# Unordered token scatters, expert tokens and rows on GpSimd's DMA queue, and first weights staged in the K and V tiles

## The chip, the cores and the metric

The kernel runs on one core of a Trainium2 chip. A core has five engines that run side by side, each with its own instruction queue, which it works off in order: TensorE (PE, matrix multiplication), VectorE (DVE), ScalarE (ACT), GpSimd (POOL) and SyncE (SP, which issues DMAs). Waits between engines are made with semaphores. The metric is the device time of one execution in microseconds; a smaller time is better. The kernel before was run three times: 2608.23, 2605.57 and 2600.91 us, median 2605.57.

## The reference

One layer of a perceiver works on 512 tokens of width 512, in three parts, each with a layer norm ahead of it and a residual sum behind it:

```python
x = x + xattn(layernorm(x), ctx_1024)   # 16 heads of 64, 512 queries, 8192 keys
x = x + attn(layernorm(x))              # Mamba block (conv, scan over tokens), then an MLP of width 2048
x = x + ffn(layernorm(x))               # experts
```

The experts' part is the one at the end:

```python
logits = x @ router_w.T
top_vals, top_idx = top_k(logits, 2)           # each token goes to 2 of 16 experts
gates = sigmoid(top_vals)
h = silu(x @ gate[e]) * (x @ up[e])            # width 512
moe = sum over a token's two experts of gates * (h @ down[e])
shared = (silu(x @ sg) * (x @ su)) @ sd        # width 1024, for every token
```

## The kernel before

Every fp32 operand is split into two fp16 parts, high and low, and a product is made of three fp16 matmuls. ACT makes the high part and VectorE the low one, so each weight block costs one instruction on each of them (`split_w`, lines 176 and 177; `pieces`, lines 1094 and 1095).

**The start and the first pass of attention.** The keys and values are made in four passes of two head pairs each (`filler`, line 426), over 16 chunks of 512 context rows. In the first pass a chunk's context arrives in fp32 (`ctx_first`, line 224: two halves named `cf`, tag `p32` with three buffers), is split, written back to DRAM, and used for K of two head pairs (`kproj_units`) and V (`vproj_units`). `smax_units` makes scores of the chunk's keys with the queries and keeps their running maximum: per chunk 16 matmuls into PSUM, each emptied by ACT (line 305). Their generators lie in the list `side`, and `pump` puts one unit of them between every four units of K and V. In pass 0 the block at line 452 loads the first weights: Wk of pair 0 into `wst`, Wk of pair 1 and Wv into buffers of tag `p32`, Wq into buffers of tag `t2k`. `first_norm` (layer norm of x, transposes) and the query projections `qproj` stand behind chunk 0 (line 483). The three biases are the first loads of the program (lines 163 to 165). TensorE's order is the program's own here (a manual schedule); the other engines' order and the DMA issues are arranged by the planner of the framework, which goes by when it expects operands to be ready. The attention proper follows, with passes 1 to 3 of this filler between its matmuls, then the Mamba block and the MLP (`tail`).

The tags `k` (two buffers) and `v` (three) in the pool `L` hold the key and value blocks of the attention proper (`main_load`, line 338); the first of these loads comes at 96 us of the profiled execution.

**The experts.** When the router's choice is known, each of the 1024 (token, expert) pairs has a slot in the DRAM buffer `xd_d`: 16 blocks of 128 rows for the experts and 7 for overflow. Eight indirect DMAs on GpSimd scatter the tokens' rows (2 KB each) to their slots (line 1201). They write to one tensor, so the framework orders each behind the one before. Meanwhile TensorE works on the shared part (`ffn(..., RS, ...)`, weights `rsg`, `rsu`, `rsd` loaded at line 761 into five buffers of tag `wpm`). Then `moe` goes over 16 experts and two overflow blocks: `moe_in` loads a block of 128 tokens (`xd`, three buffers, line 1208) and transposes it, `moe_up` makes gate and up, `moe_turn` transposes the result, `moe_down` makes the rows and writes them to `y_d` (line 1257). `moe_in` of the next block stands behind `moe_up`, `moe_down` of a block behind the `moe_up` of the next. Weights come in pieces of 512 KB (`wef`, six staging buffers, line 1089), six per expert, and are split into `we` (18 buffers) and `wpm`. All of these loads and the writes to `y_d` are in SyncE's queue. At the end a branch decides on further overflow blocks (line 1280), and eight indirect DMAs on GpSimd gather the rows of each token (line 1285), which VectorE weights and adds.

Of the kernel before, what the change touches and what calls it, by code (L numbers as in the profile page):

```python
# [9 lines left out]
F32 = mybir.dt.float32  # L10
AF = mybir.ActivationFunctionType
ALU = mybir.AluOpType
# [4 lines left out]
P = 128  # L17
NQ = 512
DM = 512
NC4 = DM // P  # L20
NPAIR = 8
CH = 512
NCH = 8192 // CH
NT = CH // P
WS = 16.0
# [4 lines left out]
NPASS = NPAIR // 2  # L30
# [8 lines left out]
def perceiver_layer(ctx: ExitStack, tc: tile.TileContext, a: dict, out: bass.AP):  # L39
    nc = tc.nc  # L40
# [22 lines left out]
    y_d = scr.tile([(16 + NOV) * P, DM], F32, name="y_d")  # L63
    xd_d = scr.tile([(16 + NOV) * P, 2 * DM], F16, name="xd_d")
# [70 lines left out]
    L = R(late, "late", 1)  # L135
    sb1 = R(attn, "a1", 1)
    sb2 = R(attn, "a2", 2)
# [12 lines left out]
    for i in range(NQT):  # L150
        t = (L if i == (NPAIR - 1) % NQT else sb1).tile([P, 2, NQ], F16, name=f"qlm{i}")
# [8 lines left out]
    bq_sb = sb1.tile([P, NPAIR], F32, name="bq_sb")  # L160
    bk_sb = sb1.tile([P, NPAIR], F32, name="bk_sb")
    bv_sb = L.tile([P, NPAIR], F32, name="bv_sb")
    nc.sync.dma_start(bq_sb, a["bq"])
    nc.sync.dma_start(bk_sb, a["bk"])
    nc.sync.dma_start(bv_sb, a["bv"])
    nc.vector.tensor_scalar(bk_sb, bk_sb, WS, None, ALU.mult)

    def stage_w(src, n, tag, stage=("wst", 1), bufs=2):
        st = sb2.tile([P, NC4, n], F32, name=f"wst_{tag}", tag=stage[0], bufs=stage[1])
        nc.sync.dma_start(st, src)  # L170
        return lambda: split_w(st, n, tag, bufs)

# [7 lines left out]
    def load_w(*x, **k):  # L180
        return stage_w(*x, **k)()
# [21 lines left out]
    def qproj(p, w):  # L203
        wh, wl = w
        ps = bank_j([P, NQ], F32, f"psq{p}")
        mm3(ps, lambda i: wh[:, i, :], lambda i: wl[:, i, :], lambda i: xTh[:, i, :], lambda i: xTl[:, i, :], NC4)
        q32 = sb2.tile([P, NQ], F32, name="q32", tag="t2k", bufs=4)
        nc.scalar.activation(q32, ps, AF.Identity, bias=bq_sb[:, p : p + 1], scale=1.0 / WS)
        qh = sb2.tile([P, NQ], F16, name="qh", bufs=4)
        ql = sb2.tile([P, NQ], F16, name="ql", bufs=2)  # L210
        split_dve(qh, ql, q32)
        return qh, ql
# [74 lines left out]
    def smax_units(c, i, qh, kh, runm, wide):  # L287

        if c == 0:
            runm[i] = sb2.tile([P, 4, 2, CH], F16, name=f"runm{i}", tag=f"runm{i}", bufs=1)  # L290
        for q2 in range(2):
            sf = sb3.tile([P, 2, 2, CH], F16, name="sf", bufs=2)
            pss = []
            for qi in range(2):
                qt = 2 * q2 + qi
                for hh in range(2):
                    s = slice(hh * 64, hh * 64 + 64)
                    pool, tag = (ps_s, "pss") if wide and qi else (ps_x, "px")
                    ps = pool.tile([P, CH], F32, name="psx", tag=tag)
                    nc.tensor.matmul(ps, lhsT=qh[s, qt * P : (qt + 1) * P], rhs=kh[s, 0, :], start=True, stop=True)  # L300
                    pss.append((sf[:, qi, hh, :], ps))
                if wide and not qi:
                    continue
                for dst, ps in pss:
                    nc.scalar.activation(dst, ps, AF.Copy, scale=1.0 / (8.0 * WS))  # L305
                pss = []
                if not qi:
                    yield 406
            r = runm[i][:, 2 * q2 : 2 * q2 + 2]
            if c == 0:  # L310
                nc.vector.tensor_copy(r, sf)
            else:
                nc.vector.tensor_tensor(r, r, sf, ALU.max)  # L313
            yield 626 if wide else 406
# [111 lines left out]
    def filler():  # L426
        side = []

        def pump():
            while side:  # L430
                u = next(side[0], None)
                if u is not None:
                    yield u
                    break
                side.pop(0)

        def pass_weights(g):
            pr = (2 * g, 2 * g + 1)
            out = []
            for src, n, tag, bufs in (  # L440
                (a["Wk"][pr[0]], P, "k", 4), (a["Wk"][pr[1]], P, "k", 4), (a["Wv"][g], 256, "v", 2),
                (a["Wq"][pr[0]], P, "q", 2), (a["Wq"][pr[1]], P, "q", 2),
            ):
                w = stage_w(src, n, tag, bufs=bufs)
                yield None
                out.append(w())
            yield out[0:2], out[2], out[3:5]

        nw = None
        for g in range(NPASS):  # L450
            pr = (2 * g, 2 * g + 1)
            if g == 0:
                wk0 = load_w(a["Wk"][0], P, "k", bufs=4)
                nct = ctx_first(0)
                wk = [wk0, load_w(a["Wk"][1], P, "k", ("p32", 3), bufs=4)]
                wv = load_w(a["Wv"][0], 256, "v", ("p32", 3))
                nc.sync.dma_start(x_sb, a["x"])
                wq = [load_w(a["Wq"][p], P, "q", ("t2k", 4)) for p in pr]
            else:
                wk, wv, wq = nw  # L460
                qh = [qproj(p, w) for p, w in zip(pr, wq)]
                yield 2 * 2592
            runm = [None, None]
            ks = [[None] * NCH for _ in pr]
            for c in range(NCH):
                if c == NCH - 7 and g < NPASS - 1:
                    nws = pass_weights(g + 1)
                if c >= NCH - 7 and g < NPASS - 1:
                    nw = next(nws, None) or nw
                ct = nct  # L470
                nxt = g * NCH + c + 1
                if nxt < NPASS * NCH:
                    nct = ctx_first(nxt) if nxt < NCH else ctx_load(nxt % NCH)
                gens = [kproj_units(p, c, ct, wk[i], ks[i]) for i, p in enumerate(pr)]
                gens += [vproj_units(g, c, ct, wv, j) for j in range(2)]
                k = 0
                for n, gen in enumerate(gens):
                    for u in gen:
                        yield u
                        k += 1  # L480
                        if k % (2 if g else 4) == 0 or len(side) > 2:
                            yield from pump()
                if g == 0 and c == 0:
                    first_norm()
                    qh = [qproj(p, w) for p, w in zip(pr, wq)]
                    yield 2 * 2592
                if c == 2:
                    for p, q in zip(pr, qh):
                        qplace(p, *q)
                side += [smax_units(c, i, qh[i][0], ks[i][c], runm, g == 0) for i in range(2)]  # L490
            side += [maxrow_units(p, i, runm) for i, p in enumerate(pr)]
            if g == NPASS - 1:
                while side:
                    yield from pump()
                    yield LAST / 10
            passes[0] = g + 1
# [136 lines left out]
def tail(tc, a, out, const, scr, ident, x_sb, mlp_d, oT, y_d, xd_d, psums):  # L633
# [562 lines left out]
    oii = G.tile([P, NOV + 1], I32, name="oii")  # L1196
    nc.vector.tensor_copy(oii, oid)

    for i in range(4):
        for j in range(2):  # L1200
            nc.gpsimd.indirect_dma_start(
                out=xd_d[:], out_offset=bass.IndirectOffsetOnAxis(ap=sg[:, j, i : i + 1], axis=0),
                in_=xf[:, i].rearrange("p x d -> p (x d)"), in_offset=None,
            )

    def moe_in(k):
        xd = g2.tile([P, 2, NC4, P], F16, name="xd", bufs=3)
        nc.sync.dma_start(xd, xd_d[k * P : (k + 1) * P, :].rearrange("t (x d m) -> t x d m", x=2, d=NC4))
        pt = bank_j([P, 2, NC4, P], F16, "pxd")
        for x in range(2):  # L1210
            for d in range(NC4):
                nc.tensor.transpose(pt[:, x, d, :], xd[:, x, d, :], id16)
        xk = g2.tile([P, 2, NC4, P], F16, name="xk", bufs=2)
        nc.scalar.copy(xk, pt)
        return xk
# [30 lines left out]
    def moe_down(k, gT, ws):  # L1246
        py = acc(k % 4)
        for c in range(NC4):
            for n, (x, y) in enumerate(((0, 0), (0, 1), (1, 0))):
                nc.tensor.matmul(  # L1250
                    py, lhsT=gT[:, x, c, :],
                    rhs=ws[4 + c // 2][:, y, (c % 2) * 512 : (c % 2) * 512 + 512],
                    start=c == 0 and n == 0, stop=c == 3 and n == 2,
                )
        yo = g2.tile([P, DM], F32, name="myo", tag="yo", bufs=4)
        nc.scalar.activation(yo, py, AF.Copy, scale=IW)
        nc.sync.dma_start(y_d[k * P : (k + 1) * P, :], yo)

    def moe(ks, weights):
        xk = moe_in(ks[0])  # L1260
# [101 lines left out]
```

## Time and profile before

| | value |
|---|---|
| median of three runs | 2605.57 us |
| the profiled execution | 2611.01 us, span 2609.3 us |
| mean granted TensorE clock | 0.973 |
| TensorE busy (matmul) | 2383.2 us, 91% |
| VectorE, ACT busy | 2062.4 us (79%), 1949.2 us (75%) |
| GpSimd busy | 44.3 us (2%), 58 instructions |
| SyncE's DMA queue | 523.69 MB, 65.8% of 16 engines' span |
| GpSimd's DMA queue | 4.20 MB, 0.5% |
| eight scatters, first start to last start | 2352.8 to 2384.1 us |
| experts, first transposed token to last result | 2399.6 to 2586.6 us |

The profile is of one execution. Its span runs from the first to the last instruction, and its device time is 1.7 us longer. A share of busy time is an average over stages with different limits; what a change in one stage is worth must be read from that stage. In the timelines, a row gives start and duration in us, the engine, the line of the kernel, the operation, output and input, and in brackets the idle time before it with what ended it. `SPq` rows are issues of DMAs by SyncE: their duration is the time of issuing, not of the transfer. A row of the windows view gives, for a stretch of time, the busy us of PE, weight loads, DVE, ACT and POOL, then the granted TensorE clock, the share of busy time of the DMA engines and the GB/s they moved.

### The profile page before, as it was taken

Reading aid. Unit: us, or ns where it says so; the run is one execution under the profiler, and the core shown is the slowest. Engines: PE = TensorE matmul, PEld = TensorE weight load, DVE = VectorE, ACT = ScalarE, POOL = GpSimd, SP = SyncE. Lnnn points to the kernel's source line nnn. Section 1 sums busy time; section 2 is a strip of 40 time slices with the busy share of each in tenths; the row PEclk is TensorE's granted clock in tenths of the full one; section 3 lists DMA queues with packets and bytes.
Section 4 is the critical chain, followed back from the end, with each engine's and each line's share of the span. In section 5 each row is a group of like instructions: output and inputs, shape, how many; then the busy total and the mean of one; then the engine's idle time right before and its main releaser. Section 6 shows DMA issues by size and latency. Waiting matters only on the chain. (4 is left out here: it accounts for less than half of the span.)

```text
span 2609.3 us, 54424 instructions
## 1 busy us (share of the span) xinstructions
PE 2383.2 (91%) x21806; PEld 1676.5 (64%) x21806; DVE 2062.4 (79%) x2403; ACT 1949.2 (75%) x3734; POOL 44.3 (2%) x58
## 2 busy tenths in 40 slices
PE   7999899999999999999999998997877688998895
PEld 3555577776677777767777777995665466665442
DVE  6776588888888888878888778997899999533785
ACT  5787788888788888868888888997776476333784
POOL 2000000000000000000000000000000000001001
PEclk9999999999999999999999999999989899999998
DMA  7974677778687778778877655877510222766896
GB/s 270 312 259 138 231 212 231 229 235 241 199 234 235 226 221 251 226 199 228 236 221 213 175 156 148 207 205 192 159 41 25 97 81 82 260 225 217 293 331 208
DMA packets 353688, 531.43 MB, mean 204 GB/s; under 512 B 25107, under 2 KB 218835, under 8 KB 353301
## 3 DMA queue, kind: packets, MB, share of 16 engines
q1 hardware_dynamic: 352148, 523.69, 65.8%
q0 software_dynamic: 1280, 4.20, 0.5%
q8 instruction: 173, 2.83, 0.5%
q14 instruction: 87, 0.70, 0.1%
HBM read 397.68 MB, written 126.94 MB: 201 GB/s over the span
## 5 line engine op out<-in xcount | busy, mean ns | idle before, releaser
L377 DVE TENSOR_TENSOR phl<-p,phl 128x1024 f16<-128x1024 f32 x512 | 626.7, 1225 | 193.2 <-ACT phl L374 181.0
L372 ACT ACTIVATE p<-pss 128x512 f32<-128x512 f32 x1024 | 597.7, 622 | 114.5 <-PE pss L365 42.2
L305 ACT ACTIVATE sf<-psx 128x512 f16<-128x512 f32 x1024 | 558.5, 625 | 70.9 <-PE psx L300 70.1
L364 PE MATMUL pss<-qhh,k 128*128 128x256 f16 x2048 | 481.0, 275 | 14.3 <-ACT phl L374 12.0
L365 PE MATMUL pss<-qlm,kb 128*128 128x256 f16 x2048 | 479.7, 274 | 0.9 <-DMA kb<-k_d 0.9
L313 DVE TENSOR_TENSOR runm<-runm,sf 128x2048 f16<-128x2048 f16 x240 | 292.3, 1219 | 51.7 <-ACT sf L305 51.5
L394 PE MATMUL po<-v,phl 128*128 128x130 f16 x4096 | 322.7, 220 | 3.9 <-DVE oq L407 3.4
L374 ACT ACTIVATE phl<-pss 128x512 f16<-128x512 f32 x512 | 312.8, 611 | 0.0
L394 PEld LDWEIGHTS <-phl 128*128 128x128 f16 x4096 | 271.0, 98 | 61.6 <-issue 14.8
L275 PE MATMUL psv<-wh_v,ctxc 128*128 128x256 f16 x1024 | 282.0, 275 | 7.3 <-ACT wh_v L176 3.2
L276 PE MATMUL psv<-wl_v,ctxc 128*128 128x256 f16 x1024 | 280.8, 274 | 1.2 <-DVE wl_v L177 1.2
L277 PE MATMUL psv<-wh_v,ctxc 128*128 128x256 f16 x1024 | 280.9, 274 | 0.0
L364 PEld LDWEIGHTS <-k 128*128 128x128 f16 x2048 | 200.9, 98 | 66.0 <-issue 20.0
L365 PEld LDWEIGHTS <-kb 128*128 128x128 f16 x2048 | 201.4, 98 | 53.0 <-issue 14.6
L300 PE MATMUL psx<-khl,qh 64*128 64x512 f16 x1024 | 208.9, 386 | 17.6 <-ACT sf L305 12.2
L922 PE MATMUL py<-hs,ident 128*128 128x256 f32 x512 | 144.0, 437 | 73.5 <-DVE hs L919 73.5
L397 PE MATMUL po<-v,phl 128*128 128x65 f16 x4096 | 208.5, 193 | 2.5 <-DVE phl L377 2.5
L251 PE MATMUL psk<-ctxc,wh_k 128*128 128x512 f16 x512 | 198.0, 387 | 9.9 <-ACT ctxc L234 8.1
L376 DVE CAST phl<-p 128x1024 f16<-128x1024 f32 x256 | 176.0, 687 | 32.2 <-ACT p L372 32.0
L252 PE MATMUL psk<-ctxc,wh_k 128*128 128x512 f16 x512 | 196.3, 383 | 0.8 <-DVE ctxc L235 0.7
L253 PE MATMUL psk<-ctxc,wl_k 128*128 128x512 f16 x512 | 196.3, 383 | 0.0
L922 PEld LDWEIGHTS py<-hs,ident 128*128 128x128 f32 x512 | 107.2, 217 | 107.0 <-DVE hs L919 87.0
(304 smaller groups left out, 3774.6 us busy)
## 6 DMA issues: line engine op xcount, KB each, us to landing
v<-v_d SPq DMA_DIRECT2D x128, 520.0 KB
k<-k_d SPq DMA_DIRECT2D x256, 256.0 KB
ctxc<-ctx_d SPq DMA_DIRECT2D x96, 512.0 KB
wef<-in_gu_dram SPq DMA_DIRECT2D x72, 512.0 KB
v_d<-vs SPq DMA_DIRECT2D x128, 260.0 KB
k_d<-khl SPq DMA_DIRECT2D x128, 256.0 KB
kb<-k_d SPq DMA_DIRECT2D x128, 256.0 KB
wpm<-w_d SPq DMA_DIRECT2D x48, 512.0 KB
```

The lines of the kernel that those rows point to most:

```text
L275: nc.tensor.matmul(ps[:, t, :], lhsT=ct[i // 2][:, 0, i % 2, sl], rhs=wh[:, i, :], start=i == 0, stop=False)
L276: nc.tensor.matmul(ps[:, t, :], lhsT=ct[i // 2][:, 0, i % 2, sl], rhs=wl[:, i, :], start=False, stop=False)
L277: nc.tensor.matmul(ps[:, t, :], lhsT=ct[i // 2][:, 1, i % 2, sl], rhs=wh[:, i, :], start=False, stop=i == NC4 - 1)
L305: nc.scalar.activation(dst, ps, AF.Copy, scale=1.0 / (8.0 * WS))
L313: nc.vector.tensor_tensor(r, r, sf, ALU.max)
L364: nc.tensor.matmul(ps[:, hh], lhsT=k[:, hh, sl], rhs=qhh[:, hh, qs], start=True, stop=False)
L365: nc.tensor.matmul(ps[:, hh], lhsT=b[:, hh, sl], rhs=qlm[:, hh, qs], start=False, stop=True)
L372: nc.scalar.activation(p32[:, i], pss[i], AF.Exp, scale=sc)
L374: nc.scalar.activation(ph[:, i], pss[i], AF.Exp, scale=sc)
L377: nc.vector.tensor_tensor(pl, p32, ph, ALU.subtract)
L394: nc.tensor.matmul(o, lhsT=ph[:, i, hh, qs], rhs=vv, start=first, stop=False, **kw)
L922: nc.tensor.matmul(py[:, j, :], lhsT=ident, rhs=hs[:, n, 1:], start=k == 0, stop=False)
```

## The change

It has three parts. The scatters are declared free of each other, and each token load waits for all eight of them. The token loads and the writes of rows are issued by GpSimd. In the start, weights are staged in the still empty buffers of the tags `k` and `v`, the bias loads move back to where the biases are first used, the context of chunk 1 is loaded in the same block, and `first_norm`, the query projections and the score units of chunk 0 move behind chunk 1.

```diff
-    nc.sync.dma_start(bq_sb, a["bq"])
-    nc.sync.dma_start(bk_sb, a["bk"])
-    nc.sync.dma_start(bv_sb, a["bv"])
-    nc.vector.tensor_scalar(bk_sb, bk_sb, WS, None, ALU.mult)
 
     def stage_w(src, n, tag, stage=("wst", 1), bufs=2):
-        st = sb2.tile([P, NC4, n], F32, name=f"wst_{tag}", tag=stage[0], bufs=stage[1])
+        pool = L if stage[0] in ("k", "v") else sb2
+        st = pool.tile([P, NC4, n], F32, name=f"wst_{tag}", tag=stage[0], bufs=stage[1])
         nc.sync.dma_start(st, src)
         return lambda: split_w(st, n, tag, bufs)
...
                 wk0 = load_w(a["Wk"][0], P, "k", bufs=4)
                 nct = ctx_first(0)
-                wk = [wk0, load_w(a["Wk"][1], P, "k", ("p32", 3), bufs=4)]
-                wv = load_w(a["Wv"][0], 256, "v", ("p32", 3))
+                wk1, wv = stage_w(a["Wk"][1], P, "k", ("k", 2), bufs=4), stage_w(a["Wv"][0], 256, "v", ("k", 2))
+                nc.sync.dma_start(bk_sb, a["bk"])
+                nc.vector.tensor_scalar(bk_sb, bk_sb, WS, None, ALU.mult)
+                nxt0 = ctx_first(1)
+                wk, wv = [wk0, wk1()], wv()
                 nc.sync.dma_start(x_sb, a["x"])
-                wq = [load_w(a["Wq"][p], P, "q", ("t2k", 4)) for p in pr]
+                wq = [stage_w(a["Wq"][p], P, "q", ("v", 3)) for p in pr]
+                nc.sync.dma_start(bq_sb, a["bq"])
+                nc.sync.dma_start(bv_sb, a["bv"])
...
                 nxt = g * NCH + c + 1
-                if nxt < NPASS * NCH:
+                if nxt == 1:
+                    nct = nxt0
+                elif nxt < NPASS * NCH:
                     nct = ctx_first(nxt) if nxt < NCH else ctx_load(nxt % NCH)
...
-                if g == 0 and c == 0:
+                if g == 0 and c == 1:
                     first_norm()
-                    qh = [qproj(p, w) for p, w in zip(pr, wq)]
+                    qh = [qproj(p, w()) for p, w in zip(pr, wq)]
                     yield 2 * 2592
+                    side += [smax_units(0, i, qh[i][0], ks[i][0], runm, True) for i in range(2)]
...
-                side += [smax_units(c, i, qh[i][0], ks[i][c], runm, g == 0) for i in range(2)]
+                if g or c:
+                    side += [smax_units(c, i, qh[i][0], ks[i][c], runm, g == 0) for i in range(2)]
+                if (g, c) == (0, 1):
+                    while len(side) > 2:
+                        yield from pump()
...
+    sent = []
     for i in range(4):
         for j in range(2):
-            nc.gpsimd.indirect_dma_start(
+            d = nc.gpsimd.indirect_dma_start(
                 out=xd_d[:], out_offset=bass.IndirectOffsetOnAxis(ap=sg[:, j, i : i + 1], axis=0),
                 in_=xf[:, i].rearrange("p x d -> p (x d)"), in_offset=None,
             )
+            for o in sent:
+                tc.declare_no_dep(d.ins, o.ins, reason="every slot is one token's: the rows differ")
+            sent.append(d)
 
     def moe_in(k):
         xd = g2.tile([P, 2, NC4, P], F16, name="xd", bufs=3)
-        nc.sync.dma_start(xd, xd_d[k * P : (k + 1) * P, :].rearrange("t (x d m) -> t x d m", x=2, d=NC4))
+        r = nc.gpsimd.dma_start(xd, xd_d[k * P : (k + 1) * P, :].rearrange("t (x d m) -> t x d m", x=2, d=NC4))
+        for o in sent:
+            tc.add_manual_dep(
+                r.ins, o.ins.name, mybir.DependencyInfo(mybir.DependencyClass.Sync, mybir.DependencyReason.DATA),
+                reason="rows of every scatter",
+            )
...
-        nc.sync.dma_start(y_d[k * P : (k + 1) * P, :], yo)
+        nc.gpsimd.dma_start(y_d[k * P : (k + 1) * P, :], yo)
```

## The prediction

> **What bounds the kernel now.** The page's first row has TensorE busy for 91% of the span, so only time in which it idles, or runs at a low clock, can be won. The chain that ended last is no help: it goes back only to the final gathers. I read instead, in this order: the waits of TensorE and of SyncE's queue from 2340 us on, the timelines of GpSimd and SyncE there, the windows by stage, and the timeline of the first 100 us.
>
> Waits (engine, line, who was waited for: us in total, times, longest):
>
> ```profile
> PE pu L703 <- DMA wpm<-rsu_d: 8.8, 1, 8.8
> ...
> PE pxd L1212 <- ACT mg L1230: 6.3, 3, 4.2
> ...
> SPq L1257 <- ACT myo L1256: 73.0, 18, 9.2
> ...
> SPq L1208 <- DMA xd_d<-xf,sg: 14.5, 1, 14.5
> ```
>
> The timelines behind them:
>
> ```profile
> 2352.83 1.15 POOL L1201 DMA_INDIRECT xd_d<-xf,sg  x1 [135.70 <-DVE sg L1184]
> 2356.02 0.97 POOL L1201 DMA_INDIRECT xd_d<-xf,sg  x1 [2.04 <-DMA xd_d<-xf,sg]
> 2362.56 0.96 POOL L1201 DMA_INDIRECT xd_d<-xf,sg  x1 [5.57 <-DMA xd_d<-xf,sg]
> ...
> 2384.12 0.95 POOL L1201 DMA_INDIRECT xd_d<-xf,sg  x1 [2.01 <-DMA xd_d<-xf,sg]
> ```
>
> ```profile
> 2372.01 0.32 SPq L761 DMA_DIRECT2D wpm<-rsg_d  x1
> 2387.22 1.31 SPq L1208 DMA_DIRECT2D xd<-xd_d  x3
> 2388.64 0.37 SPq L761 DMA_DIRECT2D wpm<-rsu_d  x1
> ...
> 2389.58 1.77 SPq L1089 DMA_DIRECT2D wef<-in_gu_dram  x3
> ```
>
> Each scatter waits for the one before to land, so eight take from 2352.83 to 2387.2. The first token load stands in SyncE's queue ahead of the last shared weights (rsu) and the next experts' weights (wef), so for 14.5 us SyncE issues nothing. The array runs out of weights at 2385.7 and restarts at 2394.48.
>
> **Scatters and token loads.** An issue costs GpSimd 0.95 us and the final gathers, which have no mutual order, follow one another every 1.26 to 1.48 us. Eight scatters then start within some 10 us and have landed by about 2368 (median landing 3.8 us, more in a burst). The token loads follow on GpSimd, about 20 us before TensorE wants them. SyncE no longer stands behind them: rsu was issued 8.2 us after the previous rsu in the turn before (2360.02, 2368.18), so it comes at about 2376.4, 9 us before its use. The 8.8 us go. The 24 matmuls behind the stall also took 0.213 us each (2394.48 to 2399.57) where warm ones take 0.109, so another 2.5 us go. **TensorE reaches the experts 11.3 us earlier.** Late next: the burst moves 2 MB while three shared blocks load; I charge 1 us for it.
>
> **The weight stream** doesn't move by as much. SyncE could issue the next expert weights when the first staged slot is free: its split on VectorE ended at 2382.5, and the issue was at 2389.58, so it gains 7.1 us. From 2389.58 to the last landing at about 2577, 90 pieces of 0.524 MB, 18 token blocks and 18 rows blocks of 0.262 MB pass: 56.6 MB in 187 us, 302 GB/s. The windows show 277, 311 and 335 GB/s in 2400-2450, 2450-2500 and 2500-2550, with TensorE busy 44.4, 45.2 and 48.5 us of 50. At 302 the end moves by 7.1 us only; at 335 all through, the stream takes 169 us and the end moves by 25. TensorE itself allows 11.3 plus the 18 us that it waits among the experts (pxd, pmg, pmt and acc rows), 29.
>
> Which of these depends on SyncE. It waits 73.0 us for ACT's copies of rows (L1256), in program order in front of weight loads; after such a wait up to five weight loads go out in a row, so their slots had been free. **Here a rule speaks against the move.** The Trainium skill ("DMA: Bandwidth & Descriptors", Issuing engines are not separate DMA queues) says that all issuers share 16 DMA engines, and a second one saves only the sequencer's issue time. By it 36 issues of 0.33 to 0.38 us are saved, 13 us of a queue that isn't the bound: nothing, and the end moves by 7.1. The row says otherwise: what is saved is the wait ahead of other loads. Bandwidth is not added, which is why 335 GB/s is the ceiling. I take the middle, 16 us, less the 1 us: **-15**.
>
> **The price on GpSimd.** No plain DMA of GpSimd is in the trace. The nearest row is its indirect DMA, 0.95 us an issue; SyncE's 0.33 us is the lower end. 36 of them are 12 to 36 us on an engine that sits idle for 206 us there. A second rule: the skill ("SBUF — State Buffer", SBUF: two separate sides, the box on VectorE blocking DMA) says that GpSimd can't write descriptors while VectorE runs a two-port mode, and VectorE is busy 40 of 50 us among the experts. By the rule, an issue there could wait out an operation of 0.7 to 1.2 us. But the scatter of 2381.15 lay beside a split on VectorE (L1095, 2381.27 to 2382.50) and took 0.95 us like the others; the expert stage has just such splits, two-input operations and copies out of PSUM. I add nothing; the rule's price is 0 to 2 us, at the end only.
>
> In GpSimd's queue a token load can stand behind the rows write of an earlier expert, which waits for ACT. There are three token buffers, so the load for expert k+3 may go once k's is transposed, an expert earlier than rows k. Covered, if that order is kept.
>
> At the end the last rows write costs GpSimd perhaps 0.95 us, landing 2.0 us later as in the scatters of 2381.15 and 2384.12: 2.97 us. SyncE's took 3.5 us (2586.59 to the gathers' release at 2590.07). GpSimd must then still take the branch, which it took at 2384.4 before. Between -0.5 and +2; I take 0.
>
> **The start.** Three bias loads leave the head of SyncE's queue: 3 x 0.46 us, everything starts 1.4 us earlier. Wv no longer waits for a context staging buffer (it was issued at 12.64). Ahead of it are then only Wk and the first context chunk, 2.1 MB with itself: at the 327 to 408 GB/s of the windows 4-8 and 8-12, about 9 us, before its use. TensorE waited 3.24 and 1.17 us for it, and ran the first matmuls behind at 0.213:
>
> ```profile
> 20.36 0.27 PE L275 MATMUL psv<-wh_v,ctxc 128*128 128x256 f16 x1 [3.24 <-ACT wh_v L176]
> ```
>
> Rebuilt from these rows: K of chunk 0 at 6.7 (8.8 us as before), V at 15.6 (48 matmuls of 0.109: 5.2), chunk 1 without score units 20.8 to 31.2, transposes 3.0, Q 5.7: 39.9. Before, Q ended at 37.2 and chunk 1, with the score units of chunk 0 between its matmuls, at 50.2. Now these 16 matmuls come alone, and ACT empties them at 0.52 us each: 8.3 us in which TensorE has only 2 us of work. Chunk 2 starts near 47.5: 2.7 us gained. Its own 17.2 us hold a wait of ACT for context (2.45 us) that an earlier load removes; against that stands the clock. After a wait for ACT and a score unit at ACT's pace, the array ran at half clock (windows; PEclk is the third number from the end):
>
> ```profile
> 80.00:82.00 2.00, 0.61 (x2) 0.18 (x2) 1.29 (x2) 2.00 (x5) 0.00 (x0) 1.00 0.94 312
> ...
> 84.00:86.00 2.00, 2.00 (x5) 0.32 (x4) 2.00 (x3) 2.00 (x6) 0.00 (x0) 0.50 0.54 214
> 86.00:88.00 2.00, 2.00 (x6) 0.55 (x5) 2.00 (x3) 2.00 (x5) 0.00 (x0) 0.50 0.79 305
> ```
>
> That costs half of some 6 us. The two about cancel; bounds -8 and +4, I take **-3**. From chunk 3 on TensorE is busy 19.5 us of 20, so the shift stays.
>
> **Sum**: -15 - 3 + 0 = -18. The profiled execution took 2611.01 us (span 2609.3), 5.4 above the median, so its 18 us are taken from the median, 2605.57: **2588 us**.
>
> **Rivals.** (1) Only the standstill goes: the stream stays at 302 GB/s (-7.1) and the start gives nothing: 2598. For it: DMA share is already 0.91 in 2500-2550, and the rule above. Against: the bursts after each rows write. (2) TensorE-bound experts, -25, with the start at -7: 2574. For it: VectorE needs 9.4 us per expert, ACT 9.2, TensorE 9.0, and shortest turns are 8.7. Against: all three at their limit at once. (3) Slower: GpSimd's order. Should each token load k+3 stand behind rows k, TensorE waits each time. The trace has one such case: rows at 2557.53, the token load at 2559.11, and a wait of 1.3 us. With 0.6 us more for each of two issues, 15 experts x 2.5 us = 37 us, against -18: 2625. It decides from 1.2 us per expert on. Against: all but this last case had the load out two experts ahead. (4) The order between scatters stays: they end at 2387 as before, but on a queue of their own; TensorE then waits some 3 us for tokens at 2388, and about 2591 results. It lies inside the forecast.
>
> **How the numbers follow.** Forecast 0.56 (with rival 4), rival 1 0.18, rival 2 0.11, rival 3 0.09, and 0.06 for a start that loses (both chunks at half clock) while the experts give little: about 2606. A measurement of this kernel tells 0.3%, 7.8 us, from no change, so rival 1 lies on the edge. Faster: 0.56 + 0.11 + half of 0.18 = 0.76, cut to 0.74 since the planner orders ACT and VectorE anew in the start; same 0.13; slower 0.13. Range: from rival 2's 2574 with 3 us for the unknown ends, 2571, to 2605, which takes in rival 1 and leaves rival 3 out.
>
> **What would show it.** Right: scatters 1.3 us apart, no gap of SyncE around 2372-2387, no wait for rsu, TensorE at the experts some 14 us earlier with the start's share, the windows among the experts above 310 GB/s, chunk 2 starting before 49 us. Wrong: waits of TensorE for xd at every expert; half clock behind the 16 score matmuls; ACT still waiting 27 us for wef.

## The result, and the profile after

The changed kernel takes 2615.73 us (median of 9 runs, 2612.36 to 2619.84) against 2605.57 us before (9 runs, 2600.85 to 2612.60): ratio 1.0038, 95% interval 1.0027 to 1.0048. It is slower by some 10 us, where 18 us less had been forecast. Timed a second time (17 runs, below) it took 2612.25 us against 2607.08: ratio 1.0026, interval 1.0017 to 1.0035. The profiled execution took 2612.45 us (span 2610.7, clock 0.974); the one of before happened to lie 5.4 us above its median, so these two executions differ by 1.4 us only, and what each stage costs has to come from the experiments.

**The scatters do what they were meant to.** The timeline of GpSimd, with the first two scatters, the last one and the first token loads:

```profile
2356.78 1.15 POOL L1211 DMA_INDIRECT xd_d<-xf,sg  x1 [135.92 <-DVE sg L1193]
2358.23 0.97 POOL L1211 DMA_INDIRECT xd_d<-xf,sg  x1 [0.30 <-issue]
...
2365.83 0.96 POOL L1211 DMA_INDIRECT xd_d<-xf,sg  x1 [0.30 <-issue]
2374.56 1.68 POOL L1221 DMA_DIRECT2D xd<-xd_d  x3 [7.77 <-DMA wpm<-rsg_d]
```

Eight of them follow one another every 1.27 us; from the first start to the last it is 9 us instead of 31. No row of TensorE's waits is for tokens, nor for `rsu`; a wait of 1.9 us for `rsg` is new. The first expert's transposes begin 37.1 us after the first scatter (2393.9) instead of 46.7.

**Among the experts the gain is lost again.** The waits from 2390 us on (engine, line, whom it waited for: us in total, times, longest), to be read beside the 73.0 us of SyncE and the 6.3 us of `pxd` before:

```profile
POOL y_d L1275 <- ACT myo L1274: 82.5, 18, 9.2
ACT we L1103 <- DMA wef<-in_gu_dram: 35.9, 34, 4.2
...
PE pxd L1230 <- ACT mg L1248: 13.2, 7, 2.6
```

The wait for rows has moved from SyncE to GpSimd, as intended. But SyncE did not become free. From 2390 to 2590 us its waits for VectorE to split a staged piece, so that the staging buffer can be loaded again, were before:

```profile
SPq L1089 <- DVE we L1095: 37.5, 35, 2.3
SPq L1089 <- DVE wpm L1095: 15.6, 20, 1.9
```

and in the changed kernel:

```profile
SPq L1098 <- DVE we L1104: 75.8, 57, 3.0
SPq L1098 <- DVE wpm L1104: 54.2, 32, 4.6
```

That is 130.0 us instead of 53.1: where 73.0 us of waits for rows went, 76.9 us of waits for buffers came. ACT waits for gate and up weights 34 times (before: 20 times, 30.3 us, of which 9.4 in one wait at the end of the standstill), and TensorE twice as long for ACT's silu (`mg`). The windows say what the supply was meanwhile (PE is the second number, the DMA share and GB/s the last two):

```profile
2450.00:2500.00 50.00, 41.70 (x243) 20.28 (x241) 41.43 (x42) 38.80 (x47) 4.87 (x9) 1.00 0.95 341
2500.00:2550.00 50.00, 43.59 (x257) 21.44 (x257) 42.51 (x44) 40.53 (x49) 5.41 (x10) 1.00 0.95 341
```

More was moved than before (311 and 335 GB/s), and TensorE did less (45.2 and 48.5 us). This points to split weights that pile up unused; they are counted below.

**At the end the gathers wait longer.** Rows of the branch at line 1298 (durations min/median/max in ns, first and last start in us), and the first gather:

```profile
L1298 POOLq EVENT_SEMAPHORE  x4: 17/43/3057, 2586.4 to 2589.6; - x4
...
L1298 POOLq INC_SWDGE_SEM  x1: 1063/1063/1063, 2589.7 to 2589.7; - x1
```

```profile
2591.93 1.01 POOL L1303 DMA_INDIRECT yg<-y_d,sg  x1 [5.74 <-issue]
```

At the branch GpSimd waits 3.06 us for its own row writes and then spends 1.06 us on an operation that the trace of before does not have. From the start of the last copy of rows to the first gather it is 7.2 us; before 5.2. Below I call this GpSimd's drain.

**The start lost.** TensorE's wait for Wv is gone and K of chunk 0 begins at 6.42 us (6.7 forecast), but chunk 2 begins at 57.4, where 50.2 was before, and chunk 3 at 72.0 instead of 67.4. The timelines of ACT and of TensorE:

```profile
48.90 9.89 ACT L302 ACTIVATE sf<-psx 128x512 f16<-128x512 f32 x20
```

```profile
38.43 1.11 PE L100 MATMUL pt_x<-ident,xn 128*128 128x128 f32 x4 [2.79 <-DVE vs L279]
...
49.54 7.92 PE L297 MATMUL psx<-khl,qh 64*128 64x512 f16 x16 [0.73 <-ACT sf L302]
57.39 0.61 PE L248 MATMUL psk<-ctxc,wh_k 128*128 128x512 f16 x1
```

Two things stand in a row: a wait of the transposes for VectorE, and twenty score matmuls, the last sixteen at the pace of ACT, which empties them one by one. Behind the wait, and again among these matmuls, the array ran at half clock (third number from the end), so that the transposes and the first half of the q-projection are slow and chunk 2 begins with a matmul every 0.42 us instead of 0.22:

```profile
38.00:42.00 4.00, 2.95 (x11) 1.94 (x12) 3.37 (x6) 1.17 (x2) 2.14 (x2) 0.50 0.96 346
...
50.00:54.00 4.00, 3.59 (x9) 0.83 (x9) 3.32 (x5) 4.00 (x9) 0.00 (x0) 0.71 0.83 288
54.00:58.00 4.00, 4.00 (x10) 0.83 (x9) 1.39 (x2) 4.00 (x10) 0.00 (x0) 0.50 0.63 186
```

### The profile page after: what moved, and what is told of

It is laid out like the page before. It is cut to its first block, busy times and chain, and to the rows that moved or that the text cites. A ratio compares the mean times of both kernels' runs of the same rounds, so it can differ in the third digit from the quotient of the medians.

```text
span 2610.7 us, 54437 instructions
## 1 busy us (share of the span) xinstructions
PE 2383.9 (91%) x21806; PEld 1677.1 (64%) x21806; DVE 2061.8 (79%) x2403; ACT 1949.4 (75%) x3734; POOL 62.5 (2%) x94
## 5 line engine op out<-in xcount | busy, mean ns | idle before, releaser
L391 PEld LDWEIGHTS <-phl 128*128 128x128 f16 x4096 | 271.7, 98 | 61.8 <-issue 14.8
L297 PE MATMUL psx<-khl,qh 64*128 64x512 f16 x1024 | 213.4, 388 | 18.1 <-ACT sf L302 12.2
L394 PEld LDWEIGHTS <-phl 128*128 128x128 f16 x4096 | 171.6, 97 | 4.3 <-DVE phl L374 3.6
```

The lines of the kernel that those rows point to most:

```text
L391: nc.tensor.matmul(o, lhsT=ph[:, i, hh, qs], rhs=vv, start=first, stop=False, **kw)
L394: nc.tensor.matmul(o, lhsT=pl[:, i, hh, qs], rhs=vv_, start=False, stop=last, **kw)
```

## The experiments

Times are medians; each ratio is against runs of the kernel before on the same chip.

### Halves and parts of the change

The change was cut at the end of the router: `s1` has only its start, `s2` only the scatters, tokens and rows. `s3` and `s4` are `s2` with one or two queues put back:

```diff
  s3: both lines, s4: the second only
-        r = nc.gpsimd.dma_start(xd, ...)
+        r = nc.sync.dma_start(xd, ...)
-        nc.gpsimd.dma_start(y_d[k * P : (k + 1) * P, :], yo)
+        nc.sync.dma_start(y_d[k * P : (k + 1) * P, :], yo)
```

s1, the start alone: 

> The start of the change alone; the experts as before. Theory A (the start costs: in the trace of the changed kernel chunk 2 begins at 57.5 us instead of 50.2 and the shift is still 6.6 us at 235 us): 2605.6 + 6.6 = 2612, between 2609 and 2616. Theory B (the start's shift is swallowed later, since other stages differ by as much, and the experts are the whole loss): 2605.6, within 2.

s2, the experts' part alone: 

> The start as before; scatters unordered, tokens and rows on GpSimd. Theory A (the experts gain a little, what the start loses is more): the traces give the experts 5.7 us of lead plus 4.0 us of shift undone at their first token, of which about 5 us are left at the gathers, less 1.8 us of drain at the branch: 2602, between 2599 and 2605. Theory B (the experts are the loss): 2612 or more. The forecast's own sum for this part was 2591.

s3, unordered scatters alone: 

> The start as before; scatters unordered, but token loads and rows stay in SyncE's queue. If the standstill of 8.8 us was the order between scatters and no more: SyncE's wait for the scatters shrinks from 14.5 us to a few, TensorE's wait for rsu goes, no drain at the branch. If GpSimd's queue is what slows the experts in the changed kernel (drain of 1.8 us, splits on ACT ahead of their weights), this is faster than the run with the experts on GpSimd: 2597. If the queue for weights matters, slower than that run: 2604.

s4, with the tokens on GpSimd too: 

> As the run with the experts on GpSimd, but rows are written by SyncE: no DMA of GpSimd is under way at the branch, so the drain of 1.8 us goes, and weight loads stand behind rows again. If the drain is the larger: 2 us faster than the run with the experts on GpSimd. If the queue of weights is the larger: slower by some us.

| kernel | median us | ratio (95%) |
|---|---|---|
| before | 2605.41 | |
| s1, start alone | 2610.09 | 1.0012 (1.0003 to 1.0021) |
| s2, experts' part alone | 2606.68 | 1.0005 (0.9995 to 1.0015) |
| s3, only scatters unordered | 2600.81 | 0.9979 (0.9969 to 0.9989) |
| s4, and tokens on GpSimd | 2599.17 | 0.9978 (0.9969 to 0.9987) |

The start costs 3 to 5 us. Free scatters are worth some 5 us, the tokens on GpSimd nothing that can be told from that, and the rows on GpSimd take it all back: 7.5 us between s4 and s2, which differ in one line. Of what was expected, s1 lies in the range of its theory A; s2 and s3 lie between their two theories; for s4 a gain of 2 us over s2 was expected, about a quarter of what came.

### What the rows do to the weights

In both kernels ACT splits the weights, and its instructions run in the order that the scheduler wrote down. I counted in that order, for each expert, how many of the 512 KB pieces are split ahead of its silu beyond those that it needs (all six of each earlier expert, its own four of gate and up): the lead. In the table it stands for the 9th, 16th and 17th of the 18 blocks, and beside it, from each profiled execution, when the last split ended (after the first scatter), how long from there to the start of the last copy of rows, and from that to the first gather.

| kernel | rows issued by | lead | last split | to last rows | to gather |
|---|---|---|---|---|---|
| before | SyncE | 8, 1, 1 | 225.5 | 7.6 | 5.2 |
| s1 | SyncE | 8, 1, 1 | 219.9 | 5.9 | 4.5 |
| s3 | SyncE | 8, 1, 1 | 216.5 | 5.9 | 4.4 |
| s4 | SyncE | 9, 5, 4 | 213.1 | 9.1 | 5.0 |
| s2 | GpSimd | 11, 9, 7 | 213.4 | 12.3 | 7.1 |
| after | GpSimd | 11, 9, 7 | 215.7 | 12.3 | 7.2 |

Before and s1 have the same expert code; their 5.6 us in the last split is what one execution differs from another. Against that, the next column repeats to 0.1 us among kernels of one lead, but for before's own 7.6. The larger the lead that is left at the 16th block, the more work lies behind the last weight. The end of ACT's timeline shows it, of the changed kernel:

```profile
2571.38 1.06 ACT L1103 ACTIVATE wpm<-wef 128x1024 f16<-128x1024 f32 x1
...
2578.01 0.60 ACT L1248 ACTIVATE mg<-pmg 128x512 f32<-128x512 f32 x1 [4.87 <-PE pmg L1243]
...
2584.76 0.60 ACT L1274 ACTIVATE myo<-acc 128x512 f32<-128x512 f32 x1 [3.40 <-PE acc L1268]
```

and of s3:

```profile
2568.06 0.60 ACT L1239 ACTIVATE mg<-pmg 128x512 f32<-128x512 f32 x1 [0.38 <-PE pmg L1234]
2568.55 1.05 ACT L1094 ACTIVATE wpm<-wef 128x1024 f16<-128x1024 f32 x1
...
2575.50 0.60 ACT L1265 ACTIVATE myo<-acc 128x512 f32<-128x512 f32 x1 [4.75 <-PE acc L1259]
```

In s3 the last weight is split after the last silu, and only one down projection is left. In the changed kernel the last block's silu comes 5.6 us after the end of the last split: TensorE still owed a block and a half. With rows on SyncE, s3 moved 324 and 343 GB/s in the two windows from 2450 to 2550 us with TensorE at 45.9 and 48.1 of 50 us; the changed kernel moved 341 in both. The supply is nearly the same. What differs is how much of it TensorE has used when it ends.

How this comes about can be seen where the silu of a block waits. ACT's timeline in the changed kernel, and TensorE's row that hangs on it:

```profile
2489.18 1.06 ACT L1103 ACTIVATE we<-wef 128x1024 f16<-128x1024 f32 x1 [1.25 <-DMA wef<-in_gu_dram]
2490.15 0.58 ACT L1248 ACTIVATE mg<-pmg 128x512 f32<-128x512 f32 x1
```

```profile
2490.78 0.61 PE L1230 MATMUL pxd<-id,xd 128*128 128x128 f16 x8 [2.01 <-ACT mg L1248]
```

TensorE has been idle since 2488.8, so the silu is ready, but a split of weights for a block almost two ahead stands in front of it, and that waits for its DMA. TensorE is held to the pace of the DMAs with ten pieces in reserve.

Rows on GpSimd change two things, the order of the weights and the queue of the rows. Two kernels take them apart. `e5` keeps the weights' order and takes the rows off GpSimd:

```diff
-        nc.gpsimd.dma_start(y_d[k * P : (k + 1) * P, :], yo)
+        nc.scalar.dma_start(y_d[k * P : (k + 1) * P, :], yo)
```

> Experts' part of the change alone (start as before), but each expert's rows are written from ScalarE's DMA queue instead of GpSimd's; SyncE carries only weights, as in the change. Theory 'lead': the rows' wait on SyncE had let TensorE catch up with the weights; without it the scheduler puts the splits of weights almost two experts ahead of the present expert's silu, ten pieces of lead stay unspent until the last two experts, and they are worked off after the last weight has landed. In this program ten pieces still lie ahead at the 16th expert, so: last split about 213 us after the first scatter, 12 us from there to the last row copy, only GpSimd's drain before the gathers (2.4 us) gone: 2604 us (2602.5 to 2605.5). Rival 'GpSimd's queue': the loss is its own (late landings, the drain); then this equals the version with rows on SyncE, 2599 to 2600.5 us, and 6 to 9 us from the last split to the last row copy.

`e6` keeps the rows on GpSimd and makes SyncE wait for them all the same:

```diff
         nc.gpsimd.dma_start(y_d[k * P : (k + 1) * P, :], yo)
+        nc.sync.dma_start(z_d[k : k + 1, :], yo[0:1, :])
```

> Experts' part of the change alone, rows on GpSimd's queue as in the change, and beside each of them a 2 KB write of one of its rows to an unused buffer in DRAM, issued by SyncE: SyncE waits for every expert's rows again, though GpSimd carries them. In program order the lead falls from 17 pieces to 4 at the 17th expert, as where SyncE writes the rows. Theory 'lead': 9 us from the last split to the last row copy instead of 12, the drain before the gathers stays (7 us from last row copy to first gather): 2602 us (2600 to 2603.5). Rival 'GpSimd's queue': nothing is gained by a wait that is added: 2606.5 us or more (2606 to 2609).

| kernel | median us | ratio (95%) | lead | last split | to last rows | to gather |
|---|---|---|---|---|---|---|
| e5, rows by ACT | 2609.19 | 1.0009 (1.0000 to 1.0017) | 11, 10, 7 | 219.1 | 12.3 | 4.1 |
| e6, a useless write by SyncE | 2601.30 | 0.9988 (0.9980 to 0.9996) | 9, 5, 4 | 210.4 | 9.1 | 7.5 |

The rival falls on both: without GpSimd's queue nothing comes back, and 18 added transfers with a wait each make the kernel 4 to 5 us faster than s2 (4.4 by the ratios, 5.4 by the medians). The two columns on the right obey the two theories separately: 12.3 or 9.1 by the order of the weights, 7 or 4 to 5 by whether GpSimd carries the rows. e6 against s4, with the same order and one queue different, puts the price of GpSimd's rows at 2 to 3 us.

One thing is not taken apart: e6 makes SyncE wait at run time, and with that the planner also orders ACT's splits anew. No run has the old order without the wait, so which of the two saves the time is open; the columns follow the order.

Two remainders I cannot place. e5 was expected at 2604 and came 5 us later; in its profiled execution all of that lies ahead of the last split (219.1). And e6 gained 3 us in its last split beside the 3.2 behind it. One execution differs from another by as much.

### What the start loses

`e8` is s1 without the last three lines of the change, which empty the list of score units behind chunk 1:

```diff
-                if (g, c) == (0, 1):
-                    while len(side) > 2:
-                        yield from pump()
```

> Start's part of the change alone, without its last lines, which empty the list of score units behind chunk 1 before chunk 2 begins; the scores of chunks 0 and 1 then come between chunk 2's units. Theory 'burst': 20 score units in a row, paced by ScalarE's copies at half clock, delay chunk 2 by 8 us; interleaved they don't, chunk 2 begins about 49 to 51 us: 2603 to 2606 us. Rival 'staging': the start is late for the order of the transfers and splits before it; then chunk 2's k is written as late as with the change (63 to 64 us): 2609 to 2611 us.

`e9` is s1 with the staging of weights kept, and normalisation, q-projection and scores back behind chunk 0:

```diff
-                if g == 0 and c == 1:
+                if g == 0 and c == 0:
                     first_norm()
                     qh = [qproj(p, w()) for p, w in zip(pr, wq)]
                     yield 2 * 2592
-                    side += [smax_units(0, i, qh[i][0], ks[i][0], runm, True) for i in range(2)]
```

> Start's part of the change alone, with its staging of the first weights in the K and V tiles and its late biases, but with normalisation, q-projection and scores behind chunk 0 again, as before the change. Theory 'burst': what loses is the work moved behind chunk 1, so this is no slower than before: 2602 to 2606 us. Rival 'staging': what loses is the staging and the order of the loads: 2608 to 2612 us.

e8 took 2604.63 us (ratio 0.9998, 0.9987 to 1.0008), e9 2613.08 (1.0025, 1.0014 to 1.0036). So emptying the list costs 4 to 5 us (s1 to e8: 3.6 by the ratios, 5.5 by the medians), and without it the start is level with before. In e8 chunk 2 begins at 46.5 us already, but chunk 3 at 67.6, as before (67.4): the scores now take their time inside chunk 2. Its window of 54 to 58 us, to be held against that of the changed kernel:

```profile
54.00:58.00 4.00, 3.66 (x15) 1.15 (x15) 1.68 (x3) 4.00 (x9) 0.00 (x0) 1.00 0.71 215
```

ACT is just as full (4.00 of 4), but chunk 2's matmuls lie between the scores and the clock stays at 1.00. e9 missed: the theory that only the moved work loses is wrong. With staging and the old order the start is 7 to 8 us slower than before. Its loss shows later, at chunk 5 (106.0 us, before 99.7), where ACT waits for context:

```profile
87.84 1.04 ACT L231 CAST ctxc<-cf 128x1024 f16<-128x1024 f32 x1 [3.53 <-DMA cf<-in_ctx_dram]
```

ACT waited 13.0 us for context in its first 120 us, against 5.3 before and 6.8 in e8. That this wait is the cause was not tested, nor why the loads come later there. The staging pays only with q behind chunk 1, and then just breaks even.

### Both repairs together

`e10` is the changed kernel with e8's and s4's edits: the list not emptied, rows by SyncE. `e11` is the changed kernel again, beside it.

> The changed kernel with two edits: the lines that empty the list of score units behind chunk 1 are left out, and the experts' rows are written by SyncE again (tokens stay on GpSimd's queue, scatters stay unordered). By the two theories ('burst' at the start, 'lead' at the experts) the start is then at before's pace (2604.6 against 2605.2 us by itself) and the experts keep their gain (2599.2 us by itself): 2598.5 us, 2595 to 2602. If the two halves hinder each other, as the changed kernel's 2615.7 us against a sum of 2611.6 would allow, it stays above 2602.5.

> The changed kernel as it is, beside the other on the same chip. Its halves by themselves cost 4.9 (start) and 1.5 us (experts), with intervals of some 2.5 us each. If halves add up: 2611.6 us, 2609 to 2614. If they hinder each other: 2615.7 us again, above 2614.

e10 took 2597.36 us (6 runs) against 2607.08: ratio 0.9963, interval 0.9951 to 0.9976. It is 9.7 us faster than before and 14.9 faster than the changed kernel at 2612.25; both came within what was expected. In its profiled execution 9.1 us lie between last split and last rows, and 5.1 to the gather, as in s4. The ratio of the changed kernel is now 1.0026; the halves' 1.0012 and 1.0005 make 1.0017, so they add up within the intervals. Of the first measurement's 1.0038 some 5 us would be left over; that stays open.

## Why the prediction was wrong

**Right.** The standstill goes. TensorE reached the experts 9.7 us after the scatters' start earlier than before; 11.3 was forecast. Scatters 1.27 us apart, no wait for `rsu`, tokens long there: rivals 3 and 4 did not happen. The 1 us charged for late loads is the 1.9 us for `rsg`. A token load or rows write costs GpSimd 0.54 us an issue, within the 0.33 to 0.95 assumed, and the issue time shows no cost of the second rule weighed there, that VectorE can hold up GpSimd's descriptors: 0.54 us each beside a VectorE busy 41 to 43 of 50 us. For the landing it is open: GpSimd's rows landed 4.9 us after the issue (median), the last four 2.3 to 3.8, when the weight loads had all but ended.

**The step that failed** is the weight stream: "I take the middle, 16 us, less the 1 us: -15". It had two parts, 7.1 us for an earlier begin and some 9 us for a faster pace. The earlier begin came: the stream began 31.4 us after the first scatter instead of 36.8, 5.3 us earlier. The faster pace did not. From its first load to the last split the stream took 184.2 us, against 188.8 in the profiled execution of before, but s1, e8 and e9, which have before's expert code, took 183.2 to 183.8, and s2 182.3 (e5 and e6, at 189.2 and 178.8, show how far single executions spread). SyncE's 73.0 us for ACT's rows were read as a cost of the queue; taken away, they came back as waits for staging buffers. So the last weight was split 9.9 us earlier than in the profiled execution of before, but only 4.3 earlier than in s1's.

What was left out altogether is the work behind the last weight. I took the end of the stream for the end of the experts, with TensorE free to follow it, and did not ask how far TensorE would be when the stream ends. It was 4.7 to 6.4 us further behind than before, and the drain took 2.0 to 2.7. From the first scatter to the first gather this is 3.2 us better than before's execution and 4.9 worse than s1's; the runs of s2 put it at +1.3 us where -15 was forecast.

In that step I also weighed the rule against the row and trusted the row too far. The skill's rule ("DMA: Bandwidth & Descriptors", Issuing engines are not separate DMA queues) was the better guide: moving rows to another issuer bought no time. The waits for rows, with the order of splits that comes with them, had let TensorE use up its reserve: with the wait put back in e6, and no transfer of use added, the kernel gains 4 to 5 us.

**The start** was forecast at -3 and measured at +3 to +5 us (s1). The warning was in the text, half clock behind 16 score matmuls, and "the two about cancel" was its wrong term: chunk 2 was to start near 47.5 and started at 57.4 us. Of those 10 us, the q-projection ended at 48.2 instead of 39.9, after a wait of 2.8 us for VectorE and in part at half clock, so 8 us were lost ahead of the scores already; the scores then took 9.2 us where 7.6 were counted (the text's own 8.3 would have put chunk 2 at 48.2). In e8 the q-projection ends at 46.5 us, as in s1 (46.6), so what lies between these two comes from the interleaving alone.

**The end** was forecast at 0, bounds -0.5 and +2, and came out at about +2: the drain at the branch was priced by the landing of a scatter, 2.97 us with its issue, where the last rows took 3.8, and without the 1.06 us behind it.

Rival 3 had the right sign and the wrong mechanism; that it lay nearer to the truth than the forecast is luck. The small case, a start that loses while the experts give little, is the one that happened, and it was given 0.06 (and 2606 us; it took 2612 to 2616).

## What to carry to other kernels

Where a stage is bound by a stream of weights, its end is the end of the stream plus the work that is then still owed. A change that lets loads run ahead gains only as far as the compute can spend that reserve before the last load lands; count, in the in-order program of the engine that prepares the weights, how many pieces lie ahead of the last blocks. And before a wait is taken off a load queue, ask which wait stands behind it, and whether it is what keeps the queue from outrunning its consumer.

## What the runs showed of the hardware

GpSimd issued a plain DMA of 256 KB in 0.54 us; SyncE took 0.33 us for the same rows (before, s3), ACT 0.33 (e5). With plain DMAs in its queue, GpSimd has an operation at the branch that before and s3 lack: 1.06 us where it writes rows (changed kernel, s2, e6), 0.72 us where it only loads tokens (s4, e5), where it came 49 us ahead of the gathers and held up nothing.

The DMA engines were not at their limit at 335 GB/s, the ceiling of the prediction: 341 at a share of 0.95 here, 358 in one window of s2 (0.97).

The clock fell to 0.50 in a stretch where TensorE had no long pause: sixteen score matmuls in 7.92 us, the wait ahead of them 0.73. The Trainium skill ("TensorE: Matmul & The Clock Gate", Part 1: The HAM clock gate) says that the gate follows how busy TensorE has been recently, and its table ties the half clock to an idle window of about 3.4 us. Here no pause was that long; a thin feed, one matmul per 0.5 us, went with the fall, and with matmuls of the next chunk in between (e8, the same 54 to 58 us) the clock stayed at 1.00.
